# Graph attention with edge types on one core: the spread of segment maxima in four products a step, its parts added on VectorE

## The chip, the cores and the metric

The kernel runs on one core of a Trainium2 chip. Its engines are TensorE (PE, with PEld for its weight loads), VectorE (DVE), ScalarE (ACT), GpSimd (POOL) and SyncE (SP, which here only issues DMAs). The metric is the device time of one execution in microseconds, the median of several.

## The reference

A graph has 3125 nodes with 128 features and 100000 edges, sorted by destination; each edge has one of 5 types. For every type `r` there is multi-head attention with 8 heads of 16 features over the edges of that type that end in a node:

```
q = x[dst] @ W_Q[r];  k = x[src] @ W_K[r];  v = x[src] @ W_V[r]
logits = (q * k).sum(-1) / 4 + attn_bias[r]          # per edge and head
max_v  = segment_max(logits of type r, dst)
exp_l  = exp(logits - max_v[dst])                    # 0 for the other types
attn   = exp_l / (segment_sum(exp_l, dst)[dst] + 1e-12)
out   += segment_sum(attn * v, dst)
```

Behind it come the output projection, a residual and a layer norm with gamma and beta, then once more a residual and a plain layer norm.

## The kernel before

A first part (until some 130 us) builds three tables in DRAM. `kv_d` has a row of keys and values for each node and type, `q_d` a row of queries for each node and type, held as three bf16 parts whose sum is the f32 value, and `key_d` holds for every edge its row in a window: 5 times (destination minus the first destination of its group) plus its type.

The main part takes the edges in 196 groups of 512, as 128 partitions times T = 4. The 512 edges of a group end in at most 25 neighbouring nodes, so a window of 125 rows (25 nodes x 5 types) holds all queries and all maxima that the group needs. `spot` (L738) makes on POOL the one-hot matrix `hot` of a group: 125 rows by 512 edges in bf16, 1 where the edge has that row. A product with `hot` as the weights spreads a window's rows to the edges.

A group is worked on twice, in a loop over steps `k` that is written out by hand:

- As a group `g`: `gather` fetches the 512 rows of `kv_d` by four indirect DMAs that POOL issues (L681), into one of 21 buffers `kv`; `spread_q` (L747) makes the queries of the edges, `qe`, by 12 products (4 columns of edges x 3 parts); `logits` (L760, L761) multiplies them with the keys, adds over each head on VectorE and stores the result.
- As a group `v`, 16 to 19 steps later, when the maxima of its nodes are known: `maxima` takes for a block of 128 nodes the largest logit per node, type and head and stores it in `m_d`, again as three bf16 parts; `fetch_m` loads the window's 125 rows of `m_d` into `mw`; `spread_m` (L864) brings the maxima to the edges, `me` in PSUM; `less_max` (L873) subtracts them from the logits, `exps` (L877, ScalarE) takes the exponential, `weigh` (L882, VectorE) multiplies the values in `kv` with it, `weights` (L890, ScalarE) copies it behind them, and `sums` (L916 and on) adds over the edges of each row by products with a second one-hot `at`. `norm` divides, `by_node` collects, `project` and the norms finish a block of nodes.

In a step POOL issues the four gathers of group `k + 2` and then makes the one-hot of group `k + 2`; once in about eight steps the load of logits for a block's maxima (L773) stands between. TensorE does, in this order, `spread_m` for the next step, `sums`, and `spread_q` for the next step. VectorE does `weigh`, `less_max` for the next step, `norm`, `logits`, and then what there is of queries, maxima and norms. A buffer `kv` is written again when the `weigh` of its group 21 groups earlier is over, and a one-hot's buffer (21 of them) when that group's `spread_m` is.

`spread_m(g, times)` makes several equal copies of the result: the window's 8 maxima are repeated `times` times along the columns of the product, 8 times while there are still groups to fetch and 12 times in the steps behind the last group; only the first copy is read. Three products a column of edges, one for each bf16 part, are added in PSUM. `live["mde", g]` is a view of that first copy in PSUM; `less_max` and `exps` work on it in place and `weigh` and `weights` read it there.

A second, general path stands behind a test of the input and isn't run for these inputs.

Of the kernel before, what the change touches and what calls it, by code (L numbers as in the profile page):

```python
# [8 lines left out]
F32 = mybir.dt.float32  # L9
# [3 lines left out]
ALU = mybir.AluOpType  # L13
AX = mybir.AxisListType
# [3 lines left out]
P = 128  # L18
# [4 lines left out]
HEADS = 8  # L23
# [17 lines left out]
T = GE // P  # L41
# [5 lines left out]
WR = WN * R  # L47
# [67 lines left out]
def block_of(g, ends=tuple(P * (b + 1) for b in range(NT))):  # L115

    return min(
        b for b, n in enumerate(ends)
        if n >= N or E // N * n - slack(n) >= min(E, (g + 1) * GE)
    )  # L120
# [12 lines left out]
def windowed_path(  # L133
# [4 lines left out]
    nc = tc.nc  # L138
# [213 lines left out]
    live = {}  # L352
# [12 lines left out]
    def fetch_keys(g):  # L365
        kt = ahead.tile([P, T, P], BF16, name="kt")
        nc.sync.dma_start(kt.rearrange("w t p -> w (t p)"), key_d[g].partition_broadcast(P))
        live["kt", g] = kt

    def fetch_q(g):  # L370
        qw = ahead.tile([P, 3, H], BF16, name="qw")
        f = window(g, first5, SPE)
        nc.sync.dma_start(qw.rearrange("w s h -> w (s h)"), q_d[bass.ds(f, P), :])
        live["qw", g] = qw
# [298 lines left out]
    ps = ctx.enter_context(tc.tile_pool(name="ps", bufs=2, space=PSUM))  # L673
    buffers(i for i in range(KVB) if i not in at_once)
    hold = ctx.enter_context(tc.tile_pool(name="hold", bufs=HELD))
    flow = ctx.enter_context(tc.tile_pool(name="flow", bufs=2))
# [10 lines left out]
    def fetch_x(name, b):  # L687
        n = min(P, N - b * P)
        xb = flow.tile([P, H], F32, name=name, bufs=2 if name == "xq" else 3)
        if n < P:  # L690
            nc.vector.memset(xb, 0.0)
        nc.sync.dma_start(xb[:n], x[b * P : b * P + n, :])
        live[name, b] = xb
# [6 lines left out]
    def turned(b):  # L700
        live["xT", b] = xT = flow.tile([P, P], F32, name="xTq", bufs=1)
        nc.scalar.copy(xT, live.pop("tp"))
        live["q3", b] = flow.tile([P, R, 3, H], BF16, name="q3", bufs=1)
# [6 lines left out]
    def first_part():  # L710
        pr, q3, n = live["pr"]
        nc.scalar.copy(q3[:, :, 0, :], pr)
# [7 lines left out]
    def second_part():  # L720
        rem, q3 = live["rem"]
        nc.scalar.copy(q3[:, :, 1, :], rem)
# [5 lines left out]
    def store_q(b):  # L728
        live.pop(("xT", b))
        nc.sync.dma_start(  # L730
            q_d[b * P * R : (b + 1) * P * R, :].rearrange("(p r) c -> p (r c)", r=R),
            live.pop(("q3", b)).rearrange("p r s h -> p (r s h)"),
        )
# [117 lines left out]
    def fetch_m(g):  # L851
        mw = late_flow.tile([P, 2, 3, HEADS // 2], BF16, name="mw", bufs=4)
        f = window(g, first5, SPE)
        nc.sync.dma_start(mw.rearrange("w h s k -> w (h s k)"), m_d[bass.ds(f, P), :])
        live["mw", g] = mw


    def spread_m(g, times):

        me = ps.tile([P, T, times, 2, HEADS // 2], F32, name="me", tag="me")  # L860
        hot, mw = live.pop(("hot", g)), live.pop(("mw", g))
        for t in range(T):
            for s in range(3):
                nc.tensor.matmul(  # L864
                    me[:, t], hot[:, t, :],
                    mw[:WR, None, :, s, :].to_broadcast([WR, times, 2, HEADS // 2]),
                    start=(s == 0), stop=(s == 2),
                )
        live["mde", g] = me[:, :, 0].rearrange("p t h k -> p t (h k)")

    def less_max(g):
        mde = live["mde", g]
        nc.vector.tensor_tensor(mde, live.pop(("lg", g))[:, :, :HEADS], mde, op=ALU.subtract)  # L873

# [14 lines left out]
    def weights(g):  # L889
        nc.scalar.copy(live["wv", g][:, :, H:], live.pop(("mde", g)))  # L890
# [37 lines left out]
    def carry(g):  # L928
        if g < NGR - 1:
            pt = late_flow.tile([WR, PW], F32, name="pt")  # L930
            nc.scalar.copy(pt, live["pp", g])  # L931
            live["pt", g] = pt
# [15 lines left out]
    def by_node(g):  # L948
        f = window(g, first, ACTE)
        nc.scalar.copy(oT[:, bass.ds(f, WN)], live.pop(("op", g)))  # L950
# [18 lines left out]
    def residual(b):  # L969
        n = min(P, N - b * P)  # L970
        if ("mv", b) not in live:
            live["mv", b] = pair()
            nc.vector.memset(live["mv", b], 0.0)
        xb = live["xr", b]
        nc.vector.tensor_tensor(xb[:n], xb[:n], beta_t[:n], op=ALU.add)
        h = late_flow.tile([P, H], F32, name="h", bufs=3)
        nc.vector.tensor_tensor(h[:n], live.pop(("pj", b))[:n], xb[:n], op=ALU.add)
        moments(live["mv", b][:, 0, :], h[:n], n)
        live["h", b] = h
# [34 lines left out]
    def store_z(b):  # L1014
        n = min(P, N - b * P)
        nc.sync.dma_start(out[b * P : b * P + n, :], live.pop(("z", b))[:n, :])
# [6 lines left out]
    group_at = {k: g for g, k in step_of.items()}  # L1023
# [10 lines left out]
    at_k, k = {}, 0  # L1034
    for v in range(NGR):
        k = max(k + 1, ready[block_of(v, MEND)])
        at_k[v] = k
    v_at = {k: v for v, k in at_k.items()}
# [24 lines left out]
    for k in range(-2, root_at[NT] + 2):  # L1063
        v, g = v_at.get(k), group_at.get(k)
        q_step = {k - f: b for b, f in enumerate(q_from) if b >= QB and -2 <= k - f <= 5}

        if k >= 0 and k + 3 in group_at:
            fetch_keys(group_at[k + 3])
            fetch_q(group_at[k + 3])
        if -2 in q_step:  # L1070
            fetch_x("xq", q_step[-2])
        for b in range(NT):
            if done_at[b] - 1 == k:
                fetch_x("xr", b)
            if norm_at[b + 1] + 1 == k:
                store_z(b)
        if 5 in q_step:
            store_q(q_step[5])
        for u in range(NGR):
            if max(at_k[u] - 3, ready[block_of(u, MEND)] - 2) == k:  # L1080
                fetch_m(u)

        for b in range(NT):
            if done_at[b] + 1 == k:
                residual(b)
        if v_at.get(k - 4) is not None:
            by_node(v_at[k - 4])
        if v_at.get(k - 2) is not None:
            carry(v_at[k - 2])
        if 1 in q_step:  # L1090
            turned(q_step[1])
        if 3 in q_step or 4 in q_step:
            second_part()
        if 2 in q_step or 3 in q_step:
            first_part()

        if v_at.get(k + 1) is not None:
            spread_m(v_at[k + 1], 8 if k + 1 in group_at else 12)
        if v_at.get(k - 1) is not None or v_at.get(k - 3) is not None:
            sums(v_at.get(k - 1), v_at.get(k - 3))  # L1100
        if k + 1 in group_at:
            spread_q(group_at[k + 1])

        if v is not None:
            weigh(v)
        while gathered < NGR - 1 and step_of[gathered + 1] <= k + AHEAD:
            gathered += 1
            gather(gathered)
        for b in range(NM):
            if full_step[b] + 1 == k:  # L1110
                maxima_load(b)
        if v_at.get(k + 1) is not None:
            less_max(v_at[k + 1])
            exps(v_at[k + 1])
        if v is not None:
            weights(v)
        if k + 1 in group_at:
            types(group_at[k + 1])
        if v_at.get(k - 2) is not None:
            norm(v_at[k - 2])  # L1120
        if g is not None:
            logits(g)
            store_logits(g)
        if k + 2 in group_at:
            spot(group_at[k + 2])
        if v_at.get(k + 1) is not None:
            places(v_at[k + 1], 2 if k >= final - 1 else 0)
        if 3 in q_step or 4 in q_step:
            third_part()
        if 2 in q_step or 3 in q_step:  # L1130
            remainder()
        for b in range(NM):
            whole = MB[b][2] is None
            last = ready[b] - (3 if whole else 4)
            if last - 2 == k and whole:
                maxima(b, 0, 2)
            if last - 1 == k and whole:
                maxima(b, 2, 4)
            if last == k:
                maxima(b, 4 if whole else 0, R)  # L1140
                store_m(b)
        for b in range(NT):
            if done_at[b] == k:
                project(b)
        for b in range(NT + 1):
            if root_at[b] == k:
                roots(b)
            if norm_at[b] == k:
                norms(b)
        if 0 in q_step:  # L1150
            turn_q(q_step[0])
        if 1 in q_step:
            queries(q_step[1], 0, RH)
        if 2 in q_step:
            queries(q_step[2], RH, R)
# [505 lines left out]
```

## Time and profile before

| what | value |
|---|---|
| time of the kernel, median of 3 runs | 1506.07 us (1504.7 to 1506.73) |
| the profiled execution: its own time | 1506.07 us |
| its span, first to last instruction | 1504.3 us |
| mean granted clock of TensorE | 0.686 |
| busy: PE, PEld | 1005.8, 800.1 us |
| busy: DVE, ACT, POOL | 901.7, 637.9, 1123.9 us |
| chain that ended last, by engine | POOL 36%, PE 26%, issue 15%, DVE 11%, DMA 7% |

Busy time leaves out what an engine spends on issuing, so a POOL that does nothing but issue indirect DMAs one after the other does not come to 100%. The profile calls a wait "issue" when nothing that it records ended it. In a group of the profile, `out<-in` are tile names, then shapes (partitions x elements), the number of instructions, the busy time in us, the mean in ns, and the idle time of the engine just before them with what ended it. The starts of matmuls are recorded, their ends are modelled. A line of the timeline has the start, the length, the engine, the line, the operation and the tiles, and in brackets the idle time before it.

### The profile page before, as it was taken

The page shows a single profiled execution, that of the slowest core. Times are in us where ns is not written, and L with a number is a line of the kernel's source. Part 1 is how long each engine was busy: PE and PEld are TensorE (multiplying, and loading weights), DVE is VectorE, ACT ScalarE, POOL GpSimd, SP SyncE. Part 2 cuts the span into 40 slices and gives each one's busy share as a digit, 9 for nine tenths or more (in the row PEclk, how much of TensorE's full clock was granted, in tenths as well). Part 3 has the DMA queues.
Part 4 walks back from the last instruction along what each step waited for, and adds up shares of the span by engine and source line. Part 5 has one row for each costly group of instructions (what it writes and reads, how often), then busy time and mean ns, then how long its engine had stood idle before and what let it go on. Part 6 is the DMA issues. An engine that isn't in the chain of part 4 may idle for free.

```text
span 1504.3 us, 26147 instructions
## 1 busy us (share of the span) xinstructions
PE 1005.8 (67%) x7526; PEld 800.1 (53%) x7526; DVE 901.7 (60%) x2365; ACT 637.9 (42%) x2248; POOL 1123.9 (75%) x1095
## 2 busy tenths in 40 slices
PE   7961336576676767667677677666776767667775
PEld 3530235455565645556565555555655555556664
DVE  5531446366557666656756665665765665566486
ACT  2540123344444454544544454444445444444354
POOL 2446788888888888888888888888888888888600
PEclk9975556566566677666767766767666776755688
DMA  6873544554554554455555545455545545444300
GB/s 184 317 255 96 143 132 122 141 139 119 146 135 128 141 139 127 132 148 128 126 146 136 127 140 140 122 145 138 135 125 144 137 125 142 130 132 120 98 17 16
DMA packets 180892, 203.66 MB, mean 135 GB/s; under 512 B 83207, under 2 KB 146083, under 8 KB 180620
## 3 DMA queue, kind: packets, MB, share of 16 engines
q0 software_dynamic: 40896, 113.39, 26.5%
q1 hardware_dynamic: 135414, 83.80, 22.7%
q10 hardware_dynamic: 4430, 4.71, 1.3%
q8 instruction: 63, 1.03, 0.3%
q14 instruction: 89, 0.73, 0.2%
HBM read 166.50 MB, written 35.28 MB: 134 GB/s over the span
## 4 chain that ended last, share of the span: by engine, by line
POOL 36%; PE 26%; issue 15%; DVE 11%; DMA 7%; another core or an unknown queue 2%; SPq 1%; ACT 1%; DVEq 0%; POOLq 0%; ACTq 0%
POOL kv L681 22%; POOL hot L738 14%; PE qe L747 6%; PE pp L916 6%; PE me L864 5%; DMA kv<-kv_d,idx 5%; PE pr L395 3%; DVE lg L761 2%; DVE prod L760 1%; PE prq L707 1%; PE pp L918 1%; PE pp L925 1%; DMA mw<-m_d 1%; POOL ell L773 1%
## 5 line engine op out<-in xcount | busy, mean ns | idle before, releaser
L681 POOL DMA_INDIRECT kv<-kv_d,idx x784 | 761.4, 971 | 227.6 <-issue 172.0
L747 PE MATMUL qe<-qw,hot 125*128 125x128 bf16 x2352 | 248.9, 283 | 435.1 <-POOL hot L738 393.1
L747 PEld LDWEIGHTS <-hot 125*128 125x128 bf16 x2352 | 202.8, 130 | 461.1 <-POOL hot L738 424.1
L916 PE MATMUL pp<-wv,at 128*125 128x136 f32 x1568 | 407.1, 402 | 0.0
L916 PEld LDWEIGHTS pp<-wv,at 128*125 128x125 f32 x1568 | 312.3, 272 | 69.4 <-issue 69.1
L738 POOL TENSOR_SCALAR hot<-kt,row_of 125x512 bf16<-125x512 bf16 x194 | 308.9, 1592 | 14.3 <-DMA kt<-key_d 8.4
L873 DVE TENSOR_TENSOR me<-lg,me 128x32 f32<-128x32 f32 x196 | 38.3, 195 | 357.0 <-PE pp L916 135.5
L877 ACT ACTIVATE me<-me 128x32 f32<-128x32 f32 x196 | 35.7, 182 | 486.2 <-issue 332.2
L902 ACT ACTIVATE at<-row_at,nkey 128x125 f32<-128x125 f32 x744 | 237.5, 398 | 0.0
L760 DVE TENSOR_TENSOR prod<-kv,qe 128x512 f32<-128x512 f32 x196 | 132.9, 678 | 63.5 <-PE qe L747 25.4
L864 PE MATMUL me<-mw,hot 125*128 125x64 bf16 (+1 forms) x2352 | 149.3, 229 | 24.9 <-DMA mw<-m_d 14.9
L864 PEld LDWEIGHTS <-hot 125*128 125x128 bf16 x2352 | 137.0, 123 | 51.5 <-issue 36.5
L882 DVE TENSOR_TENSOR wv<-kv,me 128x512 f32<-128x512 f32 x196 | 132.8, 677 | 23.2 <-remote 14.0
L761 DVE TENSOR_REDUCE lg<-prod 128x32 f32<-128x512 f32 x196 | 134.4, 686 | 6.7
L905 ACT ACTIVATE at<-at 128x500 f32<-128x500 f32 (+1 forms) x196 | 117.3, 599 | 6.2
L918 PE MATMUL pp<-pt,carried 125*5 125x136 f32 x390 | 100.7, 351 | 1.1 <-ACT pt L931 0.9
L811 DVE TENSOR_TENSOR wl<-by_head,shut 128x1024 f32<-128x1024 f32 (+2 forms) x73 | 76.9, 1053 | 12.7 <-ACT by_head L788 10.2
L925 PEld LDWEIGHTS pp<-rsum,o 125*128 125x128 f32 x392 | 80.9, 250 | 4.2 <-issue 4.1
L817 DVE TENSOR_REDUCE mx<-wl 128x16 f32<-128x1024 f32 (+2 forms) x73 | 76.5, 1048 | 2.5
L925 PE MATMUL pp<-rsum,o 125*128 125x25 f32 x392 | 71.6, 266 | 4.0 <-DVE o L940 4.0
L950 ACT COPY oT<-pp 128x25 f32 x196 | 33.8, 172 | 86.4 <-remote 32.1
L395 PE MATMUL pr<-wkv,xT 128*128 128x512 f32 x150 | 60.8, 547 | 3.6 <-issue 3.1
(185 smaller groups left out, 987.3 us busy)
## 6 DMA issues: line engine op xcount, KB each, us to landing
kt<-key_d SPq DMA_DIRECT2D x196, 128.0 KB
qw<-q_d SPq DMA_DIRECT2D x196, 96.0 KB
kv_d<-kvs SPq DMA_DIRECT2D x24, 640.0 KB
kv<-kv_d,idx POOLq DMA_INDIRECT x784
q_d<-q SPq DMA_DIRECT2D x22, 480.0 KB
lg_d<-lg SPq DMA_DIRECT2D x196, 18.0 KB
mw<-m_d SPq DMA_DIRECT2D x196, 6.0 KB
xr<-in_x SPq DMA_DIRECT2D x24, 64.0 KB
```

The costliest lines, as they stand in the source:

```text
L681: nc.gpsimd.indirect_dma_start(out=kv[:, t, :], out_offset=None, in_=kv_d[:, :], in_offset=bass.IndirectOffsetOnAxis(ap=idx[:, t, g : g + ...
L738: on.tensor_scalar(hot, live.pop(("kt", g))[:WR], row_of[:WR], None, op0=ALU.is_equal)
L747: nc.tensor.matmul(qe[:, t, :], hot[:, t, :], qw[:WR, s, :], start=(s == 0), stop=(s == 2))
L760: nc.vector.tensor_tensor(prod, kv[:, :, :H], live.pop(("qe", g)), op=ALU.mult)
L761: nc.vector.tensor_reduce(lg[:, :, :HEADS], prod.rearrange("p t (k d) -> p t k d", d=HD), AX.X, ALU.add)
L864: nc.tensor.matmul(me[:, t], hot[:, t, :], mw[:WR, None, :, s, :].to_broadcast([WR, times, 2, HEADS // 2]), start=(s == 0), stop=(s == 2),)
L882: nc.vector.tensor_tensor(wv[:, :, :H].rearrange("p t (k d) -> p t k d", d=HD), kv[:, :, H:].rearrange("p t (k d) -> p t k d", d=HD), live ...
L902: nc.scalar.activation(at[:, t, :], row_at[:, :WR], AF.Abs, bias=nkey[:, t, g : g + 1], scale=1.0)
L905: nc.scalar.activation(at[:, on_dve:], at[:, on_dve:], AF.Relu, bias=1.0, scale=-1.0)
L916: nc.tensor.matmul(pp, at[:, t, :], wv[:, t, :], start=(t == 0), stop=(t == T - 1))
L918: nc.tensor.matmul(pp[:R], carried[:WR, g, :], live.pop(("pt", g - 1)), start=False, stop=False,)
L925: nc.tensor.matmul(op, live.pop(("o5", done)), rsum[:WR], start=True, stop=True)
```

## The change

`spread_m` gets a second form, used where `times` is under 8, and the loop now asks for 5 copies while there are still groups to fetch (12 in the tail as before). In this form the three bf16 parts of the maxima aren't added in PSUM: the 24 columns of a window row (2 halves x 3 parts x 4 heads) are taken together and repeated 5 times, so that each of the 4 columns of edges takes one product of 120 columns in place of three of 64. `less_max` then adds the three parts of the first copy on VectorE, by a `tensor_reduce` from PSUM into a new tile `mde` in SBUF. What follows (the subtraction, the exponential, the weighing and the copy) works on that tile. The order of the steps and the calls in them stay as they are; `spot`, `gather`, every DMA and the pools of the other tiles are not touched.

```diff
     def spread_m(g, times):
 
+        hot, mw = live.pop(("hot", g)), live.pop(("mw", g))
+        if times < 8:
+            me = ps.tile([P, T, times, 2, 3, HEADS // 2], F32, name="me", tag="me")
+            for t in range(T):
+                nc.tensor.matmul(
+                    me[:, t], hot[:, t, :],
+                    mw[:WR, None].to_broadcast([WR, times, 2, 3, HEADS // 2]),
+                    start=True, stop=True,
+                )
+            live["parts", g] = me[:, :, 0].rearrange("p t h s k -> p t h k s")
+            return
         me = ps.tile([P, T, times, 2, HEADS // 2], F32, name="me", tag="me")
-        hot, mw = live.pop(("hot", g)), live.pop(("mw", g))
         for t in range(T):
...
     def less_max(g):
+        if ("parts", g) in live:
+            mde = flow.tile([P, T, 2, HEADS // 2], F32, name="mde")
+            nc.vector.tensor_reduce(mde, live.pop(("parts", g)), AX.X, ALU.add)
+            live["mde", g] = mde.rearrange("p t h k -> p t (h k)")
         mde = live["mde", g]
         nc.vector.tensor_tensor(mde, live.pop(("lg", g))[:, :, :HEADS], mde, op=ALU.subtract)
...
         if v_at.get(k + 1) is not None:
-            spread_m(v_at[k + 1], 8 if k + 1 in group_at else 12)
+            spread_m(v_at[k + 1], 5 if k + 1 in group_at else 12)
```

## The prediction

> **What bounds the kernel now.** I read five views in this order: the page's slices, the busy time by stage, the groups by line, the waits, and then the timeline of a few steps. In the page's slices POOL is the only row that stands at 8 from the first tenth to the last; TensorE (PE) swings between 6 and 7.
>
> ```profile
> PE   7961336576676767667677677666776767667775
> POOL 2446788888888888888888888888888888888600
> ```
>
> The busy time of the stretch 160 to 1420 us says the same. The first column is the stretch, the second its length, then each engine's busy time with its instructions.
>
> ```profile
> core 0: us, PE busy (x) PEld busy (x) DVE busy (x) ACT busy (x) POOL busy (x), PEclk, DMA share, GB/s
> 160.00:1420.00 1260.00, 851.70 (x6641) 696.31 (x6641) 773.44 (x1977) 553.27 (x1960) 1043.91 (x957) 0.67 0.52 134
> ```
>
> 83% looks as if POOL had room. The groups by line, with shapes kept apart, say that it has none:
>
> ```profile
> L681 POOL DMA_INDIRECT kv<-kv_d,idx x784 | 761.4, 971 | 227.6 <-issue 172.0 <-DMA kv_d<-kvs 13.6 <-DMA kv<-kv_d,idx 7.9
> L738 POOL TENSOR_SCALAR hot<-kt,row_of 125x512 bf16<-125x512 bf16 x194 | 308.9, 1592 | 14.3 <-DMA kt<-key_d 8.4
> L864 PE MATMUL me<-mw,hot 125*128 125x64 bf16 x2124 | 135.2, 231 | 16.6 <-DMA mw<-m_d 14.5 <-issue 1.9
> L873 DVE TENSOR_TENSOR me<-lg,me 128x32 f32<-128x32 f32 x196 | 38.3, 195 | 357.0 <-PE pp L916 135.5 <-PE me L864 122.8 <-PE pp L925 58.1
> ```
>
> Most idle time of POOL before a gather is "issue": a gap of about 0.30 us between two gathers, 0.17 behind a one-hot, 0.03 before one, in which it waits for nobody. A step of POOL is thus one one-hot (1.59), four gathers (4 x 0.97) and 1.11 of gaps: 6.58 us. In the timeline the steps from 160 to 1420 us are mostly 6.57 to 6.62 us long, some 7.8 where the load of logits at L773 is added, and no gap is over 0.31 us. POOL runs without a break from its 10th one-hot to its last, so in these 1260 us the end moves only if POOL's own instructions get longer or shorter. The waits agree:
>
> ```profile
> PEld L747 <- POOL hot L738: 424.1, 191, 6.7
> PE qe L747 <- POOL hot L738: 393.1, 176, 6.4
> ```
>
> TensorE stands some 2.1 us a step for POOL's one-hot, and VectorE (DVE) stands 357.0 us in front of L873. After 1420 us POOL has nothing left, and an 84-us tail of TensorE, VectorE and ScalarE ends the kernel.
>
> **The change, part by part.** The sum is made against the profiled execution: 1506.07 us, its span 1504.3, 1.8 outside the span; that execution is also the median of the three. The diff touches only spread_m, less_max and one argument. The one-hots of POOL (spot, L738), their place behind the gathers, every DMA and every queue stay as they are, so whatever the title says of POOL is no part of the sum.
>
> *TensorE.* The 2124 matmuls of 64 columns are 177 steps of 12; they become 177 x 4 of 120 columns. In the timeline twelve of the old ones follow each other in 0.66 us at the half clock (0.055 each) and twelve of 128 columns at 0.107 each, so four of 120 columns take some 0.40: 0.26 us less a step, 46 us over 177 steps, and eight weight loads less. All of it lies in the 2.1 us a step in which TensorE waits for the one-hot. Worth on the path: nothing. The 19 steps of the tail take 12 copies as before and don't change.
>
> *VectorE, the added reduce.* 96 elements of PSUM a partition in, 32 out, 177 times. No such form is in the trace; nearest are L873 (32 elements, 0.195 us) and L940 (128 elements from PSUM, 0.291). I take 0.26, 46 us in all. It hides in the 357.0 us of idle time before L873; were that cover gone, it would cost 46 us. A kv buffer is written again 21 groups later, so a gather waits for the weigh (L882) of the group that held it; in the timeline that weigh has ended at least 1.6 us before its gather starts, mostly 2.5 to 8, so a weigh that comes 0.26 later (or some multiples of it, behind the three steps of maxima in which VectorE has no idle time) makes no gather wait. Behind the reduce wait the subtraction L873, ScalarE's exponential and copy, then the logits; a step's idle time takes all of them.
>
> *The place of the weights.* This is the part that costs. Before, `mde` is a view of PSUM. After, it is a tile of SBUF, so L873 and the weigh L882 (0.68 us, once a step) read both inputs from SBUF. In the trace of before no frequent VectorE instruction does that; the rare ones that do (L726, L975, L992, L996) show what it means for POOL. The timeline of one step with L726, and of one with the weigh as it is now (start, length, engine, line):
>
> ```profile
> 1243.68 1.58 POOL L738 TENSOR_SCALAR hot<-kt,row_of 125x512 bf16<-125x512 bf16 x1
> ...
> 1245.28 0.55 DVE L726 TENSOR_TENSOR q<-rem,q 128x384 bf16<-128x384 f32 x1
> ...
> 1245.44 1.26 POOL L681 DMA_INDIRECT kv<-kv_d,idx  x1 [0.18 <-DVE lg L761]
> ```
>
> ```profile
> 711.30 0.68 DVE L882 TENSOR_TENSOR wv<-kv,me 128x512 f32<-128x512 f32 x1
> ...
> 711.51 1.00 POOL L681 DMA_INDIRECT kv<-kv_d,idx  x1 [0.17 <-DVE lg L761]
> ```
>
> A gather behind a one-hot takes 1.00, also where a weigh with its PSUM operand lies across its start. Where L726 lies across the start it takes 1.26: L726 ends 0.39 after the start, so the gather loses that overhang less 0.13. At 812.99 L726 ends 0.25 after the start and the gather takes 1.12; at 704.86, 0.21 and 1.09; at 333.40, with L992, 0.27 and 1.14. The law is the same in all: a VectorE instruction with two SBUF inputs that runs when a gather starts lengthens it by its remaining run less 0.13 us. One that starts while a gather already runs costs nothing. One-hots show the other side:
>
> ```profile
> 508.17 1.65 POOL L738 TENSOR_SCALAR hot<-kt,row_of 125x512 bf16<-125x512 bf16 x1
> 508.41 0.66 DVE L996 SCALAR_TENSOR_TENSOR y<-h,sd,xr 128x128 f32<-128x128 f32 x1
> ```
>
> L996 takes 0.35 away from a one-hot and 0.66 when it starts in the first 0.55 us of one; the one-hot grows by 0.07 (1.65 against 1.585).
>
> Now the price. With a weigh at any place of a step alike, each of four gather starts in 6.6 us is hit with a mean loss of (0.68 - 0.13) squared / 2 / 6.6 = 0.023 us: 0.092 a step, 16 us in 177. Weighs are not placed evenly, so I also laid the 177 of the trace against all gather starts: where they stand now, 64 are hit, for 15.5 us; moved as a whole by anything from 0.8 us earlier to 0.8 later, the sum is 10 to 25 us (25 at 0.2 later, 23 at 0.4 to 0.6 later, 19 at 0.5 earlier). The reduce moves them later, the shorter matmuls earlier; I take 18. One-hots: a weigh stands across a start in 10% of the steps, 18 x 0.07 to 0.2 = 1 to 3 us; L873 itself (0.2 long) adds under 0.5. Sum: +20 us, from +10 to +30.
>
> The Trainium skill, "SBUF — State Buffer", section "Who interferes with whom", says that VectorE and GpSimd share a second pair of SBUF ports, that a tensor_tensor with two SBUF inputs takes its read side and blocks a GpSimd instruction that reads SBUF, and infers that descriptor generation, which writes, isn't stopped by it. By that inference only the one-hots would meet the weigh, and the sum would be some +2 us, no change. The rows above (1.26 against 1.00) decide against the inference for these gathers.
>
> **Rivals.**
> 1. *TensorE is the pace after all* (faster). The chain of waits gives it 26%. If each step were as long as TensorE's work, 46 us would go: 1460. Against it: POOL's unbroken row, and 424.1 us in which weight loads wait for the one-hot.
> 2. *The weigh does not take POOL's port* as the rare instructions do, or falls between the starts (no change): 1506 to 1509. For it: a weigh starting 0.13 us behind a gather's start is free. Against it: four kinds of instruction follow the law, and over an 8-step cycle weighs start at very different places.
> 3. *The weigh locks onto the gather behind the one-hot* (slower still). In many steps it starts about 1.05 us behind the one-hot's start and ends at 1.73, just before the gather starts at 1.76. Later by some 0.5 us in every step, it would cost about 0.35 each: 60 us, 1566. It decides from 0.15 us of delay on; but the steps with maxima keep their weighs elsewhere, so not all steps can lock.
> 4. *VectorE's 46 us are not covered*: 1552. Against it: VectorE is 61% busy in the stretch.
>
> **How the numbers follow.** Forecast (hits spread over the gathers): 1506 + 20 = 1526, chance 0.76, its own range 1513 to 1536. Rival 2: 0.12. Rivals 3 and 4: 0.05 together. Rival 1: 0.07. What a measurement of this kernel tells from no change is some 0.2%, 3 us. Faster is rival 1, 0.07; same is most of rival 2, 0.11; slower 0.82. For 8 in 10 the range takes the forecast's and the upper half of rival 2: 1507 to 1536.
>
> **What would show it.** Right: L681's mean grows from 971 to about 990 ns with single gathers up to 1.5 us, and those stand where a weigh runs across their start; one-hots stay near 1.59 with a few at 1.65 to 1.8; L747 still waits for POOL; TensorE's busy time is 40 to 60 us lower; L873's idle time shrinks by about the reduce. The tail behind the last one-hot stays 84 us. Wrong: gathers that stay at 0.96 and 1.00 under a weigh; a POOL gap over 0.31 us with a VectorE releaser (rival 4); steps shorter than 6.57 us (rival 1).

## The result, and the profile after

The changed kernel takes 1528.08 us (1524.66 to 1531.37, 4 runs) against 1506.32 us (1504.70 to 1506.73, 4 runs): 1.0146 times as long, interval 1.0121 to 1.0172, which is 18 to 26 us. Predicted were 1526, in a range of 1507 to 1536, and slower. The profiled execution of the changed kernel took 1526.61 us, its span is 1524.6, its mean granted clock 0.678.

First the two slices of the page that were shown of before, then the windows of the stretch and of the tail (columns as before), all of the changed kernel:

```profile
PE   7851346567575666677676677666765666666775
POOL 2446888888888888888888888888888888888700
```

```profile
160.00:1440.00 1280.00, 832.53 (x5223) 672.57 (x5223) 852.39 (x2155) 567.50 (x1961) 1064.13 (x956) 0.66 0.51 132
1440.00:1524.60 84.60, 56.89 (x512) 46.37 (x512) 61.74 (x231) 37.03 (x149) 3.59 (x3) 0.80 0.09 20
```

POOL still stands at 8 from the first tenth to the last, and is 83% busy in the stretch, as it was. The stretch has become longer, not emptier. The groups by line and the waits of the changed kernel:

```profile
L681 POOL DMA_INDIRECT kv<-kv_d,idx x784 | 767.7, 979 | 227.3 <-issue 191.2 <-DMA kv_d<-kvs 13.6 <-DVE wv L896 3.4
L738 POOL TENSOR_SCALAR hot<-kt,row_of 125x512 bf16<-125x512 bf16 x194 | 323.4, 1667 | 13.8 <-DMA kt<-key_d 7.8
L864 PE MATMUL me<-mw,hot 125*128 125x120 bf16 x708 | 99.9, 291 | 12.4 <-DMA mw<-m_d 8.4 <-issue 2.9 <-PE qe L747 1.1
L884 DVE TENSOR_REDUCE mde<-me 128x32 f32<-128x96 f32 x177 | 45.1, 255 | 266.4 <-PE me L864 122.5 <-PE qe L747 89.1 <-issue 31.2
L896 DVE TENSOR_TENSOR wv<-kv,mde 128x512 f32<-128x512 f32 x177 | 126.1, 712 | 34.5 <-remote 18.9 <-PE pp L939 11.0 <-issue 2.6
```

```profile
PEld L747 <- POOL hot L738: 467.6, 192, 6.7
PE qe L747 <- POOL hot L738: 437.1, 188, 6.4
```

POOL's idle time before gathers is the same to 0.3 us (227.6 before, 227.3 after). What grew is the work itself: the one-hots from 308.9 to 323.4 us, 14.5 more, and the gathers from 761.4 to 767.7, 6.3 more. From the start of the 10th one-hot (177.2 us before, 177.0 after) to the end of the last one, the unbroken row, POOL takes 1244.8 us before and 1265.7 after. That is 20.8 us, and it is the whole difference of the two executions (20.5): the tail behind it is 82.3 and 82.0 us, the gaps in the stretch sum to 213.0 and 212.7, and none is over 0.32.

In what follows, the *loss* of a one-hot is its time above 1.585 us, that of a gather its time above 0.954 (above 1.004 behind a one-hot). Each loss is put down to the VectorE instruction that runs across the start. Before, one-hots lose 1.4 us and gathers 4.1. After, one-hots lose 15.9, of which the weighs 9.6 in 20 places, the rarer instructions L726 and L975 (now L989) 4.0, and L796 and L806 another 2.3; gathers lose 10.4, of which the weighs 7.7. So the weighs make 17.3 of the 20.8 us. The rest is that the rarer instructions stand elsewhere; an unchanged kernel will show below that this alone can shift by more.

Four places in the timeline of the changed kernel show how (start, length, engine, line). A weigh that begins just before a gather:

```profile
1250.49 0.68 DVE L896 TENSOR_TENSOR wv<-kv,mde 128x512 f32<-128x512 f32 x1
1250.65 1.38 POOL L681 DMA_INDIRECT kv<-kv_d,idx  x1 [0.31 <-issue]
```

The gather takes 1.38 in place of 0.96: the weigh ends 0.52 after the gather's start, less 0.10. In 47 such places the predicted law (remaining run less 0.13) gives 7.2 us, and 7.7 are measured. A weigh that begins just behind a gather's start costs nothing:

```profile
1197.14 0.96 POOL L681 DMA_INDIRECT kv<-kv_d,idx  x1 [0.30 <-issue]
1197.16 0.70 DVE L896 TENSOR_TENSOR wv<-kv,mde 128x512 f32<-128x512 f32 x1
```

Twelve weighs stand like this one, 0.02 to 0.03 us behind the gather's start. With one-hots it is the same contest, at a higher price:

```profile
1008.58 2.10 POOL L738 TENSOR_SCALAR hot<-kt,row_of 125x512 bf16<-125x512 bf16 x1
1008.63 0.69 DVE L896 TENSOR_TENSOR wv<-kv,mde 128x512 f32<-128x512 f32 x1
```

```profile
994.10 1.59 POOL L738 TENSOR_SCALAR hot<-kt,row_of 125x512 bf16<-125x512 bf16 x1
994.27 1.08 DVE L896 TENSOR_TENSOR wv<-kv,mde 128x512 f32<-128x512 f32 x1
```

At 1008.63 the weigh begins 0.05 behind the one-hot's start, and the one-hot takes 2.10. At 994.27 it begins 0.17 behind, and now the weigh is held, to 1.08, while the one-hot takes its 1.59. Twenty weighs begin between 0.46 before a one-hot's start and 0.08 behind it, and they cost 0.18 to 0.53 us each, nearly all 0.45 to 0.53. For the eleven that begin before the start the law of the gathers holds as well, with 0.15 in place of 0.13: each of these one-hots loses what is left of the weigh at its start less 0.145 to 0.149 us. Nine of the eleven are held themselves, to 0.83 to 1.07 us, so there both engines lose. The nine that begin 0.05 to 0.08 behind the start, like the one at 1008.63, cost 0.51 to 0.53. Six begin 0.16 to 0.36 behind it; they are held themselves and the one-hots lose nothing. Those that begin over 0.8 behind it cost nothing and are not held.

### The profile page after: what moved, and what is told of

Read it like the earlier page. It is cut to its first block, busy times and chain, and to the rows that moved or that the text cites. A ratio compares the mean times of both kernels' runs of the same rounds, so it can differ in the third digit from the quotient of the medians.

```text
span 1524.6 us, 23346 instructions
## 1 busy us (share of the span) xinstructions
PE 987.7 (65%) x6110; PEld 777.2 (51%) x6110; DVE 980.6 (64%) x2542; ACT 652.0 (43%) x2248; POOL 1144.9 (75%) x1095
## 4 chain that ended last, share of the span: by engine, by line
POOL 49%; issue 19%; PE 16%; DVE 8%; DMA 5%; another core or an unknown queue 2%; SPq 1%; ACT 0%; POOLq 0%; DVEq 0%; ACTq 0%
POOL kv L681 30%; POOL hot L738 17%; PE qe L747 4%; PE pp L930 4%; DMA kv<-kv_d,idx 4%; PE pr L395 3%; POOL ell L773 1%; DVE wv L896 1%; PE pp L939 1%; PE pp L932 1%; DVE lg L761 1%; PE prq L707 1%; PE me L864 1%; DVE wl L811 1%
## 5 line engine op out<-in xcount | busy, mean ns | idle before, releaser
L681 POOL DMA_INDIRECT kv<-kv_d,idx x784 | 767.7, 979 | 227.3 <-issue 191.2
L747 PE MATMUL qe<-qw,hot 125*128 125x128 bf16 x2352 | 256.3, 289 | 478.3 <-POOL hot L738 437.1
L747 PEld LDWEIGHTS <-hot 125*128 125x128 bf16 x2352 | 208.9, 132 | 504.4 <-POOL hot L738 467.6
L930 PE MATMUL pp<-wv,at 128*125 128x136 f32 x1568 | 416.8, 410 | 0.0
L930 PEld LDWEIGHTS pp<-wv,at 128*125 128x125 f32 x1568 | 328.3, 284 | 70.7 <-issue 70.4
L738 POOL TENSOR_SCALAR hot<-kt,row_of 125x512 bf16<-125x512 bf16 x194 | 323.4, 1667 | 13.8 <-DMA kt<-key_d 7.8
L884 DVE TENSOR_REDUCE mde<-me 128x32 f32<-128x96 f32 x177 | 45.1, 255 | 266.4 <-PE me L864 122.5
L891 ACT ACTIVATE mde<-mde 128x32 f32<-128x32 f32 x177 | 40.5, 229 | 372.4 <-DVE mde L887 235.9
L896 DVE TENSOR_TENSOR wv<-kv,mde 128x512 f32<-128x512 f32 x177 | 126.1, 712 | 34.5 <-remote 18.9
L864 PE MATMUL me<-mw,hot 125*128 125x120 bf16 x708 | 99.9, 291 | 12.4 <-DMA mw<-m_d 8.4
L864 PEld LDWEIGHTS <-hot 125*128 125x128 bf16 x708 | 73.4, 138 | 40.7 <-issue 24.7
L712 ACT CAST q<-prq 128x384 bf16<-128x384 f32 (+1 forms) x44 | 18.7, 425 | 113.6 <-PE prq L707 95.8
```

The lines of the kernel that those rows point to most:

```text
L681: nc.gpsimd.indirect_dma_start(out=kv[:, t, :], out_offset=None, in_=kv_d[:, :], in_offset=bass.IndirectOffsetOnAxis(ap=idx[:, t, g : g + ...
L738: on.tensor_scalar(hot, live.pop(("kt", g))[:WR], row_of[:WR], None, op0=ALU.is_equal)
L747: nc.tensor.matmul(qe[:, t, :], hot[:, t, :], qw[:WR, s, :], start=(s == 0), stop=(s == 2))
L864: nc.tensor.matmul(me[:, t], hot[:, t, :], mw[:WR, None].to_broadcast([WR, times, 2, 3, HEADS // 2]), start=True, stop=True,)
L896: nc.vector.tensor_tensor(wv[:, :, :H].rearrange("p t (k d) -> p t k d", d=HD), kv[:, :, H:].rearrange("p t (k d) -> p t k d", d=HD), live ...
L930: nc.tensor.matmul(pp, at[:, t, :], wv[:, t, :], start=(t == 0), stop=(t == T - 1))
```

## The experiments

The theory: the two-SBUF weigh delays POOL, and nothing else of the change reaches the end. The rivals: the added reduce on VectorE delays the steps (A), or TensorE's new order of products does (B). The first four kernels ran on one chip; the kernel before took 1510.01 us there (1507.35 to 1512.45, 19 runs). The changed kernel itself was not among them. The text names rare instructions by their lines in the kernel before (L726, L796, L806, L975, L992, L996), also where a changed kernel has them on another line.

**All of the change, but with the weights in PSUM.** The reduce writes into 32 columns of the products' own PSUM bank that stay free, so weigh and subtraction read one operand from PSUM, as before.

```diff
-            me = ps.tile([P, T, times, 2, 3, HEADS // 2], F32, name="me", tag="me")
+            bank = ps.tile([P, 512], F32, name="me", tag="me")   # me: its first 480 columns
+            live["spare", g] = ...                               # its last 32
...
-            mde = flow.tile([P, T, 2, HEADS // 2], F32, name="mde")
+            mde = live.pop(("spare", g))
```

> The changed kernel with one thing undone: the tile mde that the reduce writes lies in PSUM, in the 32 columns that the products leave free in their bank, so the subtraction and the weighing have one SBUF input each, as before. The four products of 120 columns and the added reduce stay. Theory (POOL is lengthened by VectorE instructions with two SBUF inputs): back to the time before, 1506 us within 3; one-hots at a mean of 1.59 us (1.67 in the changed kernel), gathers at 0.971 (0.979). Rival A (the 45 us that the reduce adds to VectorE push the rest back): stays at 1528. Rival B (what TensorE does, its shorter products and its clock, moved the step): stays at 1528.

Measured: 1506.46 us, 0.9978 times the kernel before (0.9968 to 0.9987). Everything else of the change is still there, the 177 reduces of 0.26 us and TensorE's fewer products, and the loss is gone: rivals A and B fall. The one-hots did not come back to the expected 1.59, however (gathers and one-hots, by line):

```profile
L681 POOL DMA_INDIRECT kv<-kv_d,idx x784 | 762.1, 972 | 227.4 <-issue 181.0 <-DMA kv_d<-kvs 13.6 <-DMA kv<-kv_d,idx 7.9
L738 POOL TENSOR_SCALAR hot<-kt,row_of 125x512 bf16<-125x512 bf16 x194 | 316.3, 1631 | 10.1 <-DMA kt<-key_d 4.0
```

The one-hots lose 8.9 us, but next to nothing of it to a weigh: L726 and L975 make 6.2 of it, in 21 places, and L796 and L806 another 2.4. The weighs are harmless even where they stand worst, as here in the timeline of this kernel, 0.23 before a one-hot's start:

```profile
331.89 0.69 DVE L903 TENSOR_TENSOR wv<-kv,me 128x512 f32<-128x512 f32 x1 [0.32 <-PE pp L937]
332.12 1.59 POOL L738 TENSOR_SCALAR hot<-kt,row_of 125x512 bf16<-125x512 bf16 x1
```

26 weighs begin between 0.46 before a one-hot and 0.08 behind it in this kernel, and those one-hots lose 0.08 us together. In the changed kernel 20 did, for 9.6 us. It is the same with the gathers: 66 weighs lie across a gather's start with more than 0.13 us to run, which the law would make 12.4 us, and 0.4 are measured. The two kernels differ in nothing but the place of the weights, so the operand's memory decides, not the overlap in time.

**Only the place of the weights.** The kernel before, with the subtraction's result in SBUF in the 177 steps and nothing else of the change: no reduce, the 12 products as they were.

```diff
-        mde = live["mde", g]
-        nc.vector.tensor_tensor(mde, live.pop(("lg", g))[:, :, :HEADS], mde, op=ALU.subtract)
+        me = mde = live["mde", g]
+        if live.pop(("early", g)):
+            live["mde", g] = mde = flow.tile([P, T, HEADS], F32, name="mde")
+        nc.vector.tensor_tensor(mde, live.pop(("lg", g))[:, :, :HEADS], me, op=ALU.subtract)
```

> The kernel before with one part of the change alone: three products of 64 columns added in PSUM, no reduce, but in the 177 steps with groups to fetch the subtraction writes its result to a tile in SBUF, so that the weighing alone has two SBUF inputs (the subtraction keeps its PSUM input). Theory: slower than before by 10 to 30 us, 1516 to 1536, all of it in the lengths of one-hots and gathers; the split between them can differ from the changed kernel's 14.5 and 6.3 us, since the weighings stand elsewhere. Rivals A and B: 1506, as there is neither a reduce nor another product.

Measured: 1537.28 us, 1.0181 times the kernel before (1.0164 to 1.0198), just above what was expected, and more than the whole change costs. Its groups by line:

```profile
L681 POOL DMA_INDIRECT kv<-kv_d,idx x784 | 772.4, 985 | 227.3 <-issue 182.1 <-DMA kv_d<-kvs 13.6 <-DMA kv<-kv_d,idx 8.2
L738 POOL TENSOR_SCALAR hot<-kt,row_of 125x512 bf16<-125x512 bf16 x194 | 332.0, 1712 | 10.2 <-DMA kt<-key_d 4.1
```

The weighs take 14.9 us from the one-hots and 12.2 from the gathers. For the gathers the law gives 12.07 us in 71 places, and 12.15 are measured. In 18 places a weigh begins before a one-hot's start, and the one-hot loses what is left less 0.14 to 0.15 us. ScalarE's exponential and copy work on the SBUF tile here too, but the loss stands where the weighs do: against the trace of the kernel before on the same chip (below) POOL's unbroken row is 26.0 us longer, and 27.1 are put down to weighs. So the two-SBUF weigh alone is enough, and the law gives its price for the gathers of this kernel within 1%; what the law meets depends on where the weighs happen to stand.

**Reduce into SBUF, subtraction back into PSUM.** The weigh again reads the weights from PSUM; only the subtraction, 0.24 us long, still has two SBUF inputs.

```diff
-        mde = live["mde", g]
-        nc.vector.tensor_tensor(mde, live.pop(("lg", g))[:, :, :HEADS], mde, op=ALU.subtract)
+        of = mde = live["mde", g]
+        if ("spare", g) in live:
+            live["mde", g] = mde = live.pop(("spare", g)).rearrange("p t h k -> p t (h k)")
+        nc.vector.tensor_tensor(mde, live.pop(("lg", g))[:, :, :HEADS], of, op=ALU.subtract)
```

> The changed kernel with the reduce's result in SBUF, so that the subtraction (0.19 us) has two SBUF inputs, but with the subtraction's result in the free columns of the PSUM bank, so that the weighing (0.68 us) has one. Theory with the loss growing with what is left of the VectorE instruction when POOL's starts: 1506 to 1509, since a subtraction is too short to outlast a gather's start by more than some 0.1 us. If the mere presence of a second SBUF input costs, whatever the length: 1515 or more. Rivals A and B: 1528.

Measured: 1502.37 us, 0.9950 times the kernel before (0.9933 to 0.9967): no loss from the subtraction, none from the weigh, and 4 us under the range that was expected, so faster than the kernel before. One-hots lose 3.7 us and gathers 3.4; the first kernel's 6.2 us at L726 and L975 are 1.2 here. This surprise is taken up below.

**The weigh in four instructions.** All of the change, the weigh split by columns of edges, so that each part's remaining run is at most 0.32.

```diff
-        nc.vector.tensor_tensor(wv[:, :, :H]..., kv[:, :, H:]..., live["mde", g]..., op=ALU.mult)
+        for t in range(T):
+            nc.vector.tensor_tensor(wv[:, t : t + 1, :H]..., kv[:, t : t + 1, H:]...,
+                                    live["mde", g][:, t : t + 1]..., op=ALU.mult)
```

> The changed kernel with each weighing of 512 columns made as four of 128 in the 177 steps with groups to fetch (about 0.29 us each in place of 0.68). The same bytes come from SBUF, VectorE works 0.5 us a step more. Theory (an exclusive hold for one instruction, loss = what is left of it less 0.12 us): a gather loses at most 0.17 and a one-hot some 0.2, in place of up to 0.5 each: 1508 to 1516. If it is the amount of data read from SBUF that counts, or if POOL has to wait for a whole run of VectorE instructions: 1528 or more. Rival A: over 1528, as VectorE has still more to do.

Measured: 1511.29 us, 1.0007 times the kernel before (0.9998 to 1.0017), as expected. Its weighs by line:

```profile
L899 DVE TENSOR_TENSOR wv<-kv,mde 128x128 f32<-128x128 f32 x708 | 186.3, 323 | 5.5 <-PE pp L933 5.0 <-ACT at L922 0.3
```

The total of the weighs grows from 126.1 to 186.3 us, and yet POOL loses less: 1.9 us of gathers and 6.5 of one-hots are put down to them, 7.7 and 9.6 in the changed kernel. So VectorE's time is not what costs. How long one instruction still runs when a POOL instruction starts is.

**The kernel before, profiled again.** In the first two kernels L726 and L975 cost one-hots 6 to 7 us, in the first trace of before they did not. Was that the experiments' doing, or the chip's?

> The kernel before once more, for a trace on the chip of the other runs. The changed kernel without the SBUF tile came out 0.2 to 0.5% under the kernel before there, which no theory forecast. Theory: the rare VectorE instructions with two SBUF inputs (L726, L796, L975, L992, L996) lie across other starts of POOL in each kernel, since the steps of VectorE shift; the kernel before then loses some 10 us on this chip in one-hots and gathers, against 8.4 in the run with the weighing from PSUM. Rival (the shorter products save time at the end): the same 5.6 us of losses as in its first trace, and a tail behind the last one-hot that is longer by the difference.

Measured: 1505.67 us, one execution; 1.4 us of loss in the one-hots and 3.7 in the gathers. The expectation fell, but this run was on another chip than the four above, so the question stayed open until the second such run (below).

**A shorter POOL stretch.** If POOL's unbroken row is the bound, one-hots taken away from it should give back all of their time. Every fourth or every second one-hot (L738) is made on VectorE, where the trace of before has one at 0.35 and one at 0.46 us; first in the kernel before, then, for every second, in the kernel with the weigh from PSUM.

```diff
-        on = nc.vector if g < 2 else nc.gpsimd
+        on = nc.vector if g < 2 or g % 4 == 1 else nc.gpsimd
```

> The kernel before with every fourth one-hot made on VectorE in place of POOL (0.40 us there in the two that are made so at the start, 1.59 on POOL). If POOL sets the pace of the whole stretch, 48 steps lose 1.6 us each: 77 us less, some 1435 us with a few us of new contention. If TensorE or VectorE set the pace: no change or slower.

> The same with every second one-hot on VectorE: 97 steps lose 1.6 us each, 155 us less, 1355 us, as long as POOL alone sets the pace. TensorE is busy 852 of 1260 us in the stretch and would have 1105: where its work or VectorE's becomes the longer one in some steps, less is gained, 1370 to 1420.

> Every second one-hot on VectorE, on top of the changed kernel with the weighing from PSUM: TensorE has eight products a step less, VectorE 0.26 us a step more. If TensorE has become the longer one in the run with half of the one-hots on VectorE, this is faster than that by up to 46 us; if VectorE has, slower by up to 45; if POOL still sets the pace, the same within 5.

On this chip the kernel before took 1506.17 us (7 runs). Every fourth in the kernel before: 1492.88 us, 0.9915 (0.9893 to 0.9936), 13 us where 71 were expected. Every second in it: 1562.83, 1.0388 (1.0360 to 1.0416), a loss where 1420 at most was expected. Every second with the weigh from PSUM: 1482.29, 0.9840 (0.9818 to 0.9863). That is 80.5 us faster than the same share in the kernel before on the same chip, and none of the three expected cases goes beyond 46. The waits say what came in its place. Of the kernel before with every fourth, with every second, and of the one from PSUM with every second (us in total, times, longest):

```profile
POOL kv L681 <- DVE den L937: 47.5, 45, 3.1
```

```profile
POOL kv L681 <- DVE den L937: 179.9, 78, 6.8
DVE me L873 <- remote: 168.2, 26, 10.0
```

```profile
POOL kv L681 <- DVE mde L891: 108.0, 83, 4.8
```

POOL now waits before gathers, for a buffer kv that a weigh has not yet left: in the first of the three, 47 of the weighs end 0.27 to 0.28 us before the gather that overwrites their group's buffer. The line named is what VectorE did next behind the weigh. In the kernel before, these weighs ended at least 1.6 us ahead. So the bound passes from POOL's row to the ring of gather, weigh and 21 buffers, and 48 one-hots gave back 74.6 us of POOL's work (308.9 to 234.3) while 57 us of new gaps took most of it.

**Once more, on the chip of the first four kernels.** The kernel before and the one with the weigh from PSUM again, and then every third and every fourth one-hot on VectorE in the latter. The kernel before took 1507.96 us (14 runs).

> The kernel before a third time, beside the next runs on the same chip, for what the trace of the second one left open: it had 5.6 us of losses in one-hots and gathers, as the first, and so did not show where the 0.5% of the run with the weighing from PSUM came from.

> The changed kernel with the weighing from PSUM once more. If its 0.5% under the kernel before was the kernel's: again 0.993 to 0.997, and the trace shows it against the kernel before on the same chip as an earlier start of the unbroken stretch of POOL, a shorter stretch or a shorter tail. If it was that chip's or that hour's: 0.998 to 1.003, as POOL's one-hots and gathers are within 1 us of the kernel before.

> Weighing from PSUM, every third one-hot on VectorE. With half of them there, POOL waited some 120 us for weighings to free its buffers; with every fourth and the old products some 57. Here 65 steps lose up to 1.6 us, 104 us, and some 60 to 90 of them come back as waits for weighings: 1465 to 1485.

> Weighing from PSUM, every fourth one-hot on VectorE. 48 steps lose up to 1.6 us, 77 us; the kernel before with the same share came to 0.9915, with 57 us of waits for weighings. If the eight products fewer free the buffers earlier: 1465 to 1480; if they don't: 1490.

The kernel before, in the profile, took 1509.09 us there. By line, first it, then the one with the weigh from PSUM:

```profile
L681 POOL DMA_INDIRECT kv<-kv_d,idx x784 | 763.7, 974 | 227.4 <-issue 181.7 <-DMA kv_d<-kvs 13.6 <-DMA kv<-kv_d,idx 10.4
L738 POOL TENSOR_SCALAR hot<-kt,row_of 125x512 bf16<-125x512 bf16 x194 | 316.8, 1633 | 10.2 <-DMA kt<-key_d 4.1
```

```profile
L681 POOL DMA_INDIRECT kv<-kv_d,idx x784 | 760.2, 970 | 227.5 <-issue 183.2 <-DMA kv_d<-kvs 13.6 <-DMA kv<-kv_d,idx 8.5
L738 POOL TENSOR_SCALAR hot<-kt,row_of 125x512 bf16<-125x512 bf16 x194 | 312.1, 1609 | 10.4 <-DMA kt<-key_d 4.3
```

So the same kernel before makes one-hots of 1592 ns in one execution and of 1633 in another, though the order of instructions on POOL and on VectorE is the same in both. Of the 69 instructions L726 and L975, none begins between 0.46 before a one-hot's start and 0.08 behind it in either trace with 1592 (or 1593) ns, and 19 do in this one, with just 19 one-hots over 1.70 us. In the two executions with 1592 ns the unbroken row begins at 177 and 175 us, here at 168. That answers the open question: the first experiment's 8.9 us of one-hot losses are what the kernel before has in its one trace on that chip (9.4), not a cost of the experiment. Whether it is the chip that sets the places of these instructions, or the execution, one or two traces on each don't show.

The kernel with the weigh from PSUM takes 1501.13 us, 0.9957 (0.9941 to 0.9972), so its gain of 0.4 to 0.5% holds. Between these two traces the span falls by 8.5 us: POOL's unbroken stretch by 8.0 (one-hots 4.7 less, gathers 3.5 less), its start is 1.4 later, the tail 1.9 shorter. 7 of the 69 instructions begin in that window of a one-hot, where 19 did; and at the gathers' starts, where L726 and L996 cost 2.2 us in 16 places, they now cost next to nothing. What moved them wasn't settled. Since the trace of before on the other chip has only 5.1 us of losses in all, the gain there can be smaller; that wasn't run.

With every third one-hot on VectorE: **1405.30 us, 0.9321 times the kernel before (0.9298 to 0.9344)**, 60 us under what was expected. With every fourth: 1425.29, 0.9458 (0.9435 to 0.9481), 40 us under the lower end of its range. Every third, slices and groups by line (the last line is VectorE's share):

```profile
POOL 2547788888888788888888888888888888888500
```

```profile
L681 POOL DMA_INDIRECT kv<-kv_d,idx x784 | 757.9, 967 | 235.8 <-issue 184.8 <-DMA kv_d<-kvs 13.6 <-DMA kv<-kv_d,idx 7.8
L738 POOL TENSOR_SCALAR hot<-kt,row_of 125x512 bf16<-125x512 bf16 x130 | 208.9, 1607 | 11.0 <-DMA kt<-key_d 6.9
L738 DVE TENSOR_SCALAR hot<-kt,row_of 125x512 bf16<-125x512 bf16 x66 | 30.3, 460 | 3.3 <-DMA kt<-key_d 2.2 <-DMA kv<-kv_d,idx 1.0
```

POOL's row is unbroken again: no gap over 0.32 us in the stretch, and no wait for a weigh; every weigh ends at least 1.04 us ahead of its gather. And now the sum of POOL closes: against the same kernel without the move, one-hots fall by 103.2 us (312.1 to 208.9), gathers by 2.3, and the gaps before gathers grow by 8.3, since more gathers follow a gather (0.30) and fewer a one-hot (0.17). That is 97.2 us, and the end of the last one-hot falls from 1416.8 to 1319.6, which is 97.2. So work taken out of POOL's row, with no new wait in it, moves the end by the same amount: POOL's row sets the end here. This is also the fastest of all the kernels.

Against the kernel before with the same every fourth one-hot moved (1492.88, on the other chip), every fourth here is 67 us better, and POOL's stretch has no gap over 0.33 in place of 48. The comparison on one chip, with every second, gives the 80.5 us above. TensorE's idle time before L747 that ends with POOL's one-hot is 454.7 us with every fourth here and 209.1 in the kernel before with every fourth, so TensorE has more time left when POOL sets the pace. That the shorter spread on TensorE brings the weighs forward would fit this, but it isn't shown: the kernels differ in the reduce, in the 4 products in place of 12, and in the split of subtraction and weigh between the memories, and these weren't taken apart. Nor was every third one-hot moved in the kernel before. What is shown is that the change with the weigh from PSUM, worth at most 0.5% by itself, makes room that pays once POOL has less to do.

## Why the prediction was right, point by point

**The bound.** Right, and shown: POOL's row stays unbroken (gaps 212.7 us against 213.0), the whole loss lies in it, and taking 103 us of one-hots out of it moved its end by 97.

**TensorE worth nothing on the path.** Right: with the same products and the weights in PSUM the time is that of before. The saving itself was over-estimated: L864 went from 135.2 to 99.9 us busy, 35 where 46 were worked out from the pace of the products, and the engine's busy time from 1005.8 to 987.7 us, where 40 to 60 less were to be seen.

**The reduce.** 0.255 us was measured for 0.26, and 45.1 us for 46; it is hidden, as the experiment with the weights in PSUM shows, and L747 waits for POOL longer than before. The idle time in front of it shrank by more than the reduce, though: VectorE stands 272.5 us before the reduce and the subtraction behind it, against 357.0 before L873. Other VectorE instructions also take longer in the changed kernel, L806 and L796 by 21.7 us together and the weighs by 6.2.

**The place of the weights.** This carried the sum, and the mechanism is shown by four kernels. Its two terms were mis-sized, in opposite senses. *Gathers*, +18 us: measured +6.3. The law held (7.2 worked out from the weighs of the trace after, 7.7 measured), but the places were taken from the trace of before: 64 hits of 0.24 us in the mean were laid out there, and there were 47 of 0.16. Twelve more weighs begin just behind a gather's start and eleven up to 0.034 us before it, where they are held for a moment and the gather loses nothing. *One-hots*, +1 to +3 us: measured +14.5, of which the weighs are 9.6. The signs say the same: a mean near 1.59 and a few at 1.65 to 1.8 were forecast, and the mean is 1.667, with 32 one-hots over 1.70 and the longest at 2.11.

That 20 places were met where 18 were estimated is chance. The 18 are 10% of the steps, as if weighs stood anywhere alike; where they stand in the trace of before, only 4 lie across a one-hot's start, and 13 of the 20 are at one-hots behind the load of logits. The price of one hit was misread. The 0.07 at 508.17 was put down to L996, which begins 0.24 into that one-hot. But in the trace of before L992 runs across the same start:

```profile
507.84 0.54 DVE L992 SCALAR_TENSOR_TENSOR h<-h,mv,gamma_t 128x128 f32<-128x128 f32 x1
```

It has 0.213 us left there, and 0.213 less 0.147 is the 0.066 that the one-hot lost. It is so with all 15 one-hots that meet an L996 at 0.23 to 0.25 us: L992 lies across the start of each. L996 itself costs nothing there and is held, to 0.66. A price of 0.2 is also that of the only one-hot over 1.70 us in the trace of before:

```profile
216.19 0.83 DVE L726 TENSOR_TENSOR q<-rem,q 128x256 bf16<-128x256 f32 x1
216.67 1.78 POOL L738 TENSOR_SCALAR hot<-kt,row_of 125x512 bf16<-125x512 bf16 x1
```

L726 has 0.346 left at that start, and 0.346 less 0.147 is the 0.2. So the rows of before already held the law for one-hots, the same as for gathers, and it allows a weigh of 0.68 us up to 0.53. The prediction took the prices of instructions with little left to run as the price of a weigh. After, the weighs that meet a one-hot have mostly 0.60 to 0.75 left.

The 4.0 us at L726 and L989 and the 2.3 at L796 and L806 were in no term. The total, 20 predicted and 20.8 measured, is right by luck: the two errors cancelled, and 3.5 us of the 20.8 are not the weighs' at all. The mechanism was right, its two sizes were not.

**The rule on the shared ports.** The Trainium skill, "SBUF — State Buffer", section "Who interferes with whom", infers that a tensor_tensor doesn't stop descriptor generation. These gathers are held all the same, 1.38 us against 0.96 under a weigh with two SBUF inputs. The prediction took this to decide against the inference, but it doesn't: a gather also takes its row numbers from the SBUF tile `idx`, so what is held can be that read and not the writing of descriptors, and no run here separates the two. The same section's statement that the order of issue decides who is blocked agrees with the weigh at 994.27, which is held to 1.08 us. By the recorded starts it does not fit the one at 1008.63, which begins 0.05 us behind the one-hot and still costs it 0.51.

**The rivals.** TensorE's pace (1460) and the uncovered reduce (1552) fell with the first experiment. That the weigh takes no port (1506 to 1509) fell with the second, which is 27 us slower with nothing else changed. The lock onto one start (1566) came half true, and on the other instruction: once in some 55 us a one-hot stands behind the load of logits, and a weigh meets 13 of these 24 (at 459.40, 514.50, 569.31 and so on to 1338.73). That is at most one step of eight, not all.

## What to carry to other kernels

When an engine's operand moves from PSUM to SBUF, ask which other engine takes turns at SBUF with it: a free-looking tile cost 20 us here, and 32 spare columns of a PSUM bank took it back. Read a contention's price by how much of the other instruction is left at the start, and look at every instruction that lies across that start before you name one. Don't lay old places against a new law as if they stood still. And look at what a change without a gain makes room for: with the weigh from PSUM this one gave at most 0.5% until POOL had less to do, and then the two together gave 7%.

## What was not expected of the hardware

A VectorE instruction with two SBUF inputs and a POOL one-hot decide within a tenth of a microsecond which of them waits: begun 0.05 to 0.08 us behind the one-hot's start, the weigh costs the one-hot 0.51 to 0.53 us; begun 0.16 to 0.36 behind, it is held itself (0.90 to 1.09 us in place of 0.68). Begun over 0.8 us into the one-hot it meets nothing (0.68 to 0.69 us), so the one-hot doesn't hold it off for its whole run. With a gather the turn comes at about 0.035 us before its start. And one kernel, unchanged, had one-hots of 1592 and of 1633 ns in executions on different chips, 8 us in all, with an unbroken row that began at 175 to 177 us and at 168.
